# One TensorE task weighs both token halves of a head pair, and fewer halves are turned in 32x32 squares

## The chip, the cores and the metric

The kernel runs on one core of a Trainium2 chip. The metric is the time of one execution on the device, in microseconds (us); the time of the kernel before is the median of three runs, and beside it stands one profiled execution, whose rows are read here. Engines are named as in the profile: PE (matmuls), PEld (its weight loads), DVE, ACT, POOL, and SP, which here only issues DMAs (its queue is SPq).

## The reference, cut to what matters

Eight sequences of 512 tokens by 256 channels go through a decoder layer in float32: a linear attention with an MLP, a cross attention over a context of 512 rows by 128 channels, and a feed-forward block that picks one of eight adapters per sequence; a layer norm closes each. The change is in the cross attention only:

```python
qh = (q @ Wq).reshape(B, N, NUM_HEADS, HEAD_DIM).transpose(0, 2, 1, 3)   # 16 heads of 64
scores = jnp.einsum('bhnd,bhmd->bhnm', qh, kh) * scale                   # 512 tokens x 512 context rows
attn = jax.nn.softmax(scores, axis=-1)
out = jnp.einsum('bhnm,bhmd->bhnd', attn, vh)                            # the weighing
return out.transpose(0, 2, 1, 3).reshape(B, N, INNER) @ Wo + bo
```

## The kernel before, in words

**Tiling.** The batches run one after another, overlapped: while batch b is in cross attention, the linear attention and MLP of batch b+1 and the feed-forward block of batch b-1 fill the engines. In `cross_attention` the 16 heads are eight pairs (`pr`), and the tokens of a batch are two halves of 256 (`half`), each two chunks of 128 (`c`). A half of a pair is called a part here: there are 8 x 8 x 2 = 128 parts.

**One part** (`attend`, `soft`, `place`, `weigh`). For each chunk, PE makes the scores of the two heads (L872, 64-row operands, kind "rows"), DVE takes the maximum (L879), ACT the exponential (L887), and POOL or ACT scales by the inverse sum (L898, L896). The probabilities `p` stand with tokens on the partitions, and the weighing needs context rows there, so they are turned, in one of two ways:

- by PE: four 128x128 transposes for each chunk and head into a PSUM bank (L918, kind "full"), then a copy from the bank into `pT` by ACT (L371) or DVE (L373). A part takes 16 transposes and 4 copies;
- "in squares": DVE turns 32x32 blocks into `blk` (L908, 4 instructions a part), and 16 DMAs on SP's queue (L938, `place`) put the blocks in their places in `pT`. The list `BLOCKED` (L57 to L60) names these parts.

Then `weigh` multiplies `v2` by `pT`: for each of four context tiles and two heads one matmul with 64 output rows (L954, kind "cols"; 16 records a part, two for each matmul), into 256 columns of a bank `av`, which ACT or DVE copies to `oT` (L371, L373). `project_out` (L970) uses four pairs of `oT` at a time.

**Which parts are in squares before.** Batch 0 none; batches 1 to 3 the second half of each pair, 8 parts; batches 4 to 6 that and the first half of the odd pairs, 12 parts; batch 7 the first nine of such a list, which leaves its pairs 6 and 7 to PE. That is 24 + 36 + 9 = 69 parts; the other 59 are turned by PE. Batch 0 handles its two halves in two separate passes over the pairs (`part` is one half at a time).

**What sets the order.** Every piece of work is a `task` with an engine, an estimated cost, a due time and the buffers it reads and makes. `play` runs a model of the five engines when the program is built: whenever the model's engine is free, the ready task with the lowest due time is emitted, with a surcharge or rebate where PE changes its kind (`CHANGE`, `SWAY`). A task is ready only if a spot is free for each buffer that it makes. So each engine's order is fixed in the program, and on the chip each engine goes through its list in that order. Due times count in `PACE` = 3.2 us; a pair has eight of them in batches 1 to 7.

**The buffers around the change.** There are four one-bank PSUM buffers (`bank`), eight `p`, two `pT` and two `blk`. The second of `pT` and of `blk` shares memory with the product buffers of the linear attention (L251 to L254):

```python
room("pT", 1, [P, 2 * NT * 2 * P])
room("blk", 1, [P, 2 * NT * 2 * P])
for name, i in (("blk", 0), ("pT", 2)):
    rooms[name].append(Spot(prods[:, i * N : i * N + 2 * NT * 2 * P], tuple(rooms["prod"][i : i + 2])))
```

In the profile that memory is called `prods`, whatever lies in it; "bank<-prods,v" on L954 is a weighing from the second `pT`.

Of the kernel before, what the change touches and what calls it, by code (L numbers as in the profile page):

```python
# [18 lines left out]
P = 128  # L19
B, S, C = 8, 512, 256  # L20
NT = S // P
# [6 lines left out]
H2, D2 = 16, 64  # L28
INNER = H2 * D2
NPAIR = H2 // 2  # L30
# [21 lines left out]
PACE = 3200.0  # L52
# [2 lines left out]
WINDOWS = {1: (4, 44), 2: (44, 88), 3: (88, 138)}  # L55

BLOCKED = {  # L57
    b: [(pr, half) for pr in range(NPAIR) for half in range(2) if half or b > 3 and pr % 2] for b in range(1, B)
}
BLOCKED[B - 1] = BLOCKED[B - 1][:9]  # L60

AFTER = {6: (30, 84)}

# [5 lines left out]
def decoder(ctx: ExitStack, tc: tile.TileContext, t: dict, out: bass.AP):  # L69
    nc = tc.nc  # L70
# [45 lines left out]
    def task(  # L116
        engine, took, due, emit, reads=(), writes=(), weights=(), kind=None, slack=0.0, holds=(), after=0.0, others=(),
        two=False,
    ):
        k = Task(engine, took, due, emit, kind, slack)  # L120
        k.two = two
        k.on.update((e, (n, wait)) for e, n, wait in others)
        k.at = max([after] + [eta[n] for n in weights])
        before = {}
        for key in reads:
            writers, readers = last.setdefault(key, ([], []))
            before.update((id(d), d) for d in writers)
            readers.append(k)
        for key in writes:
            writers, readers = last.get(key, ([], []))  # L130
            before.update((id(d), d) for d in (*writers, *readers))
            last[key] = ([k], [])
        before.pop(id(k), None)
        for d in before.values():
            d.next.append(k)
        k.unmet = len(before)
        k.vals = list({id(v): v for v in (*(v for v, _ in (*reads, *writes)), *holds)}.values())
        k.makes = [v for v in {id(v): v for v in (*(v for v, _ in writes), *holds)}.values() if v.room]
        for v in k.vals:
            v.left += 1  # L140
        if not k.unmet:
            for e in k.on:
                ready[e].append(k)
        return k
# [118 lines left out]
    for spot_v in rooms["v"]:  # L263
        nc.gpsimd.memset(spot_v.t[:, D1, :], 1.0)

    eta = {"now": 2000.0 + 4.0 * S * C / 185}

    def arrive(name, shape):

# [92 lines left out]
    def mm(cols, n):  # L362

        return n * {512: 858.0, 256: 432.0, 128: 222.0}[cols]
# [4 lines left out]
    def copy(e, dst, src):  # L369
        if e == "act":  # L370
            nc.scalar.copy(dst, src)  # L371
        else:
            nc.vector.tensor_copy(dst, src)  # L373
# [93 lines left out]
    def chunks(v, cs=range(NT)):  # L467
        return [(v, (kc, c)) for kc in range(KC) for c in cs]
# [340 lines left out]
    def attend(b, x1T, ctx, pr, part, at):  # L809
        cols, cs = slice(pr * P, (pr + 1) * P), range(2 * part[0], 2 * part[-1] + 2)  # L810
        rows = slice(cs[0] * P, (cs[-1] + 1) * P)
        n = len(cs) * P
        qT, kT, v2, oT = Val("qT"), Val("kT"), Val("v2"), Val("oT")
        ps_q, ps_k, ps_v = Val("bank"), Val("bank"), Val("bank")

        def project_q():
            for kc in range(KC):
                nc.tensor.matmul(  # L818
                    ps_q.t[:, :n], Wq[:, kc, cols], x1T.t[:, kc, rows], start=kc == 0, stop=kc == KC - 1
                )  # L820

        def project_v():
            for m in range(NT):
                keys = slice(m * P, (m + 1) * P)
                nc.tensor.matmul(ps_v.t[:, keys], ctx.t[:, keys], Wv[:, 0, cols], start=True, stop=True)  # L825

        task("pe", mm(n, 2), at - 9 * PACE, project_q, chunks(x1T, cs), [(ps_q, 0)], ("Wq",), "full", holds=[qT])
        task(
            "act", 600, at - 8.8 * PACE, lambda: nc.scalar.mul(qT.t[:, rows], ps_q.t[:, :n], D2**-0.5),  # L829
            [(ps_q, 0)], [(qT, 0)],  # L830
        )
        task(
            "pe", mm(512, 1), at - 8 * PACE,
            lambda: nc.tensor.matmul(ps_k.t, Wk[:, 0, cols], ctx.t, start=True, stop=True),
            [(ctx, 0)], [(ps_k, 0)], ("Wk",), "full", holds=[kT],
        )
        task(
            "act", 590, at - 7.8 * PACE, lambda e: copy(e, kT.t, ps_k.t), [(ps_k, 0)], [(kT, 0)],
            others=[("dve", 690, 1500)],
        )  # L840
        task("pe", mm(128, 4), at - 3 * PACE, project_v, [(ctx, 0)], [(ps_v, 0)], ("Wv",), "full", holds=[v2])
        task(
            "act", 600, at - 2.5 * PACE,
            lambda e: copy(e, v2.t.rearrange("p m d -> p (m d)"), ps_v.t), [(ps_v, 0)], [(v2, 0)],
            others=[("dve", 690, 1500)],
        )
        for half in part:
            pT, base = Val("pT"), at + 4 * (half - part[0]) * PACE
            blk = Val("blk") if (pr, half) in BLOCKED.get(b, ()) else None
            for c in (2 * half, 2 * half + 1):  # L850
                soft(qT, kT, pT, blk, c, base + (0.1 * (c % 2) - 6) * PACE, base + 2 * (c % 2) * PACE)
            if blk:
                place(pT, blk, base + PACE)
            weigh(v2, pT, oT, half, bool(blk), base + 6 * PACE)
        return oT

    def by_head(pT):

        return pT.t.rearrange("p (m i n) -> p m i n", m=NT, i=2)

    def by_block(pT):

        return pT.t.rearrange("p (m g i n) -> p m g i n", m=NT, g=4, i=2)
# [65 lines left out]
    def place(pT, blk, due):  # L929

        keys = [(i, c) for i in range(2) for c in range(2)]

        def emit():
            to = pT.t.rearrange("p (m g r) -> p m g r", m=NT, g=4)
            of = blk.t.rearrange("p (m j r) -> p m j r", m=NT, j=4)
            for j in range(4):
                for g in range(4):
                    nc.sync.dma_start(out=to[32 * j : 32 * j + 32, :, g], in_=of[32 * g : 32 * g + 32, :, j])  # L938

        task("sp", 9600, due, emit, [(blk, k) for k in keys], [(pT, k) for k in keys], slack=2500)  # L940


    def weigh(v2, pT, oT, half, blocked, due):
        av = Val("bank")

        def emit():
            for m in range(NT):
                for i in range(2):
                    cols = slice(i * D2, (i + 1) * D2)
                    if blocked:  # L950
                        to, of = av.t[cols, : 2 * P].rearrange("p (g n) -> p g n", g=4), by_block(pT)[:, m, :, i]
                    else:
                        to, of = av.t[cols, : 2 * P], by_head(pT)[:, m, i]
                    nc.tensor.matmul(to, v2.t[:, m, cols], of, start=m == 0, stop=m == NT - 1)  # L954

        task("pe", 1728, due, emit, [(v2, 0)] + [(pT, (i, j)) for i in range(2) for j in range(2)], [(av, 0)], kind="cols", holds=[oT])
        def put(e):
            to, of = oT.t[:, half * 2 * P : (half + 1) * 2 * P], av.t[:, : 2 * P]
            if blocked:
                to, of = to.rearrange("p (c g n) -> p g c n", c=2, g=4), of.rearrange("p (g c n) -> p g c n", c=2, g=4)  # L960
            copy(e, to, of)

        task("act", 370, due + 0.5 * PACE, put, [(av, 0)], [(oT, half)], others=[("dve", 424, 100)])

    def project_out(x, oTs, prs, c, due):
        ps = Val("bank")
# [177 lines left out]
    with tc.manual_schedule(engines=MANUAL):  # L1144
        task("dve", 800, PERIOD, adapter_table, (), [(chosen, 0)], after=2 * eta["now"])
        for b in range(B):
            start = b * PERIOD
# [76 lines left out]
```

## Time and profile before

| what | value |
|---|---|
| median of 3 runs | 1658.99 us (1658.43 to 1659.1) |
| profiled execution | 1659.94 us, span of its records 1658.1 us |
| mean granted PE clock | 0.978 of full speed |
| DVE busy | 1321.9 us (80%) |
| ACT busy | 1055.4 us (64%) |
| POOL busy | 1020.2 us (62%) |
| transposes of `p` on PE (L918) | 944 |
| 32x32 turns on DVE (L908) | 200 + 76 = 276, mean 687 and 690 ns |
| DMAs of `place` (L938) | 480 + 320 + 176 + 128 = 1104, median 2.0 us to landing |
| copies into `pT` or its second spot | ACT 120 + 68, mean about 600 ns; DVE 28 + 20, mean about 675 ns |

276 turns are 69 parts of four, 1104 DMAs are 69 parts of 16, and 944 transposes are 59 parts of 16, as the list says. Busy time is the union of an engine's instructions; a timeline row gives start and extent of a run of like instructions, and since matmuls are pipelined the time that PE spends on one is read from start to next start.

### The profile page before, as it was taken

Reading aid. Unit: us, or ns where it says so; the run is one execution under the profiler, and the core shown is the slowest. Engines: PE = TensorE matmul, PEld = TensorE weight load, DVE = VectorE, ACT = ScalarE, POOL = GpSimd, SP = SyncE. Lnnn points to the kernel's source line nnn. Section 1 sums busy time; section 2 is a strip of 40 time slices with the busy share of each in tenths; the row PEclk is TensorE's granted clock in tenths of the full one; section 3 lists DMA queues with packets and bytes.
Section 4 is the critical chain, followed back from the end, with each engine's and each line's share of the span. In section 5 each row is a group of like instructions: output and inputs, shape, how many; then the busy total and the mean of one; then the engine's idle time right before and its main releaser. Section 6 shows DMA issues by size and latency. Waiting matters only on the chain.

```text
span 1658.1 us, 23850 instructions
## 1 busy us (share of the span) xinstructions
PE 1561.0 (94%) x7736; PEld 919.3 (55%) x7736; DVE 1321.9 (80%) x2248; ACT 1055.4 (64%) x2318; POOL 1020.2 (62%) x821
## 2 busy tenths in 40 slices
PE   5579999999999999989999999999999999999995
PEld 3446666654665556645566555555554654654562
DVE  6887996798889898959968899788989756776554
ACT  2257776678656796657765686567666577556543
POOL 6376986786669586758747595656967331443222
PEclk8779999999999999999999999999999999999998
DMA  8000000022112211221122222242222332233300
GB/s 266 1 1 1 1 1 1 7 51 52 51 31 68 67 27 32 57 77 39 38 52 63 79 55 65 60 118 70 66 77 71 95 80 64 74 106 89 90 6 30
DMA packets 176651, 94.43 MB, mean 57 GB/s; under 512 B 19936, under 2 KB 174048, under 8 KB 176528
## 3 DMA queue, kind: packets, MB, share of 16 engines
q1 hardware_dynamic: 175760, 91.32, 20.6%
q0 software_dynamic: 768, 1.60, 0.4%
q8 instruction: 62, 1.02, 0.3%
q14 instruction: 61, 0.50, 0.1%
HBM read 16.30 MB, written 4.19 MB: 12 GB/s over the span
## 4 chain that ended last, share of the span: by engine, by line
PE 64%; DVE 17%; ACT 6%; SPq 5%; issue 4%; POOL 2%; DMA 2%; DVEq 0%; POOLq 0%; ACTq 0%
PE bank L954 10%; PE sc L872 10%; PE bank L970 5%; PE bank L687 5%; SPq L938 5%; PE bank L712 5%; PE bank L918 5%; PE bank L818 4%; DVE nmax L879 4%; PE bank L514 3%; DVE o L612 3%; PE bank L825 2%; ACT p L887 2%; PE bank L992 2%; DVE kv L589 2%
## 5 line engine op out<-in xcount | busy, mean ns | idle before, releaser
L887 ACT ACTIVATE p<-sc,nmax 128x512 f32<-128x512 f32 x512 | 348.5, 691 | 127.5 <-DVE nmax L879 115.8
L898 POOL TENSOR_SCALAR p<-p,rinv 128x512 f32<-128x512 f32 x300 | 209.3, 710 | 294.5 <-DVE rinv L892 275.9
L879 DVE TENSOR_REDUCE nmax<-sc 128x2 f32<-128x1024 f32 x256 | 305.3, 1212 | 69.6 <-PE sc L872 69.3
L580 POOL TENSOR_TENSOR prods<-k,v 128x1088 f32<-128x1088 f32 x115 | 288.9, 2533 | 72.8 <-DVE k L554 38.8
L603 POOL TENSOR_TENSOR prods<-q,kv 128x1088 f32<-128x1088 f32 x107 | 266.7, 2516 | 37.6 <-DVE kv L589 24.8
L872 PE MATMUL sc<-kT,qT 64*128 64x512 f32 x1024 | 267.8, 628 | 4.1 <-ACT kT L371 1.8
L589 DVE TENSOR_REDUCE kv<-prods 128x68 f32<-128x1088 f32 x120 | 152.3, 1272 | 17.8 <-POOL prods L580 17.5
L612 DVE TENSOR_REDUCE o<-prods 128x68 f32<-128x1088 f32 x128 | 161.3, 1270 | 4.6 <-POOL prods L603 4.5
L918 PEld LDWEIGHTS bank<-ident,p 128*128 128x128 f32 x944 | 106.4, 141 | 88.9 <-issue 48.6
L896 ACT ACTIVATE p<-p,rinv 128x512 f32<-128x512 f32 x212 | 143.8, 732 | 6.2 <-DVE rinv L892 6.2
L872 PEld LDWEIGHTS sc<-kT,qT 64*128 64x128 f32 x1024 | 88.1, 188 | 105.4 <-issue 79.2
L908 DVE STREAM_TRANSPOSE blk<-p 128x512 f32<-128x512 f32 x200 | 130.9, 687 | 17.0 <-POOL p L898 9.3
L918 PE MATMUL bank<-ident,p 128*128 128x128 f32 x944 | 134.6, 278 | 9.3 <-ACT qT L829 2.6
L954 PE MATMUL bank<-pT,v 128*64 128x256 f32 x1040 | 128.2, 389 | 5.7 <-DMA pT<-blk 2.7
L954 PE MATMUL bank<-prods,v 128*64 128x256 f32 x1008 | 124.4, 389 | 6.9 <-DMA prods<-prods 6.1
L818 PE MATMUL bank<-x1T,Wq 128*128 128x512 f32 (+1 forms) x288 | 124.7, 556 | 0.8 <-ACT x1T L371 0.5
L970 PE MATMUL bank<-Wo,oT 128*128 128x256 f32 x512 | 121.1, 381 | 0.0
L712 PE MATMUL bank<-projT,h 128*128 128x256 f32 x512 | 119.0, 383 | 1.3 <-ACT kT L371 0.7
L712 PEld LDWEIGHTS bank<-projT,h 128*128 128x128 f32 x512 | 94.9, 190 | 28.1 <-issue 8.3
L970 PEld LDWEIGHTS bank<-Wo,oT 128*128 128x128 f32 x512 | 94.9, 190 | 26.9 <-issue 14.6
L687 PE MATMUL bank<-xT,fcT 128*128 128x512 f32 x224 | 105.9, 600 | 2.2 <-DVE x L717 1.1
L1111 DVE SCALAR_TENSOR_TENSOR h<-bank,decb,xT 128x512 f32<-128x512 f32 x128 | 88.9, 740 | 21.7 <-PE bank L1101 20.7
(140 smaller groups left out, 2676.8 us busy)
## 6 DMA issues: line engine op xcount, KB each, us to landing
prods<-blk SPq DMA_DIRECT2D x480, 64.0 KB, 2.0
pT<-blk SPq DMA_DIRECT2D x320, 64.0 KB, 2.0
prods<-prods SPq DMA_DIRECT2D x176, 64.0 KB, 2.0
pT<-prods SPq DMA_DIRECT2D x128, 64.0 KB, 2.0
x<-in_x SPq DMA_DIRECT2D x7, 512.0 KB, 5.3
out<-x SPq DMA_DIRECT2D x7, 512.0 KB, 3.1
ctx<-in_ctxT SPq DMA_DIRECT2D x8, 256.0 KB, 3.0
fcT<-in_fcT SPq DMA_DIRECT2D x1, 1024.0 KB, 7.7
```

The costliest lines, as they stand in the source:

```text
L580: (nc.gpsimd if e == "pool" else nc.vector).tensor_tensor(pr.t.rearrange("p (d e h) -> p d e h", d=DSPLIT, h=H1), k.t[:, s : s + DSPLIT, : ...
L603: (nc.gpsimd if e == "pool" else nc.vector).tensor_tensor(pr.t.rearrange("p (h e d) -> p h e d", h=DSPLIT, d=D1), q.t[:, s : s + DSPLIT, : ...
L612: nc.vector.tensor_reduce(o.t[:, s : s + DSPLIT, :], pr.t.rearrange("p (h e d) -> p h e d", h=DSPLIT, d=D1), AX.X, ALU.add)
L712: nc.tensor.matmul(ps.t[:, :C], of(f, c), projT[:, f, :], start=f == fs[0], stop=f == fs[-1])
L818: nc.tensor.matmul(ps_q.t[:, :n], Wq[:, kc, cols], x1T.t[:, kc, rows], start=kc == 0, stop=kc == KC - 1)
L872: nc.tensor.matmul(ps.t[:, i, :], qT.t[rows, c * P : (c + 1) * P], kT.t[rows, :], start=True, stop=True)
L879: lambda: nc.vector.tensor_reduce(nmax.t, ps.t, AX.X, ALU.max, negate=True), [(ps, 0)], [(nmax, 0)],
L887: lambda i=i, p=p: nc.scalar.activation(p.t, ps.t[:, i, :], AF.Exp, bias=nmax.t[:, i : i + 1], accum_out=ssum.t[:, i : i + 1]),
L898: nc.gpsimd.tensor_scalar(p.t, p.t, rinv.t[:, i : i + 1], 1.0, ALU.mult, ALU.mult)
L918: nc.tensor.transpose(bank.t[:, m * P : (m + 1) * P], p.t[:, m * P : (m + 1) * P], ident)
L954: nc.tensor.matmul(to, v2.t[:, m, cols], of, start=m == 0, stop=m == NT - 1)
L970: nc.tensor.matmul(ps.t[:, :C], oT.t[:, c * P : (c + 1) * P], Wo[:, pr, :], start=pr == prs[0], stop=pr == prs[-1])
```

## The change

`weigh` takes all parts of a pair that `attend` handles in one call, and is called once after the loop over halves. Its PE task holds the matmuls of both halves, one half after the other, into the two 256-column halves of one bank. It is due 6 `PACE` after the base of the last half, which is when the second half's weighing was due; its first half was due 4 `PACE` sooner. Where neither half is in squares one copy takes all 512 columns of the bank to `oT`; otherwise there are two copies of 256, as before. Batch 0, whose passes have one half each, keeps one half to a task.

`BLOCKED` loses the first halves of the odd pairs in batches 4 to 6, and batch 7 keeps the second halves of pairs 0 to 5: 6 x 8 + 6 = 54 parts in squares, and 74 turned by PE. A constant that the planner's model uses for the arrival of the weights is 2100 in place of 2000 ns.

```diff
 BLOCKED = {
-    b: [(pr, half) for pr in range(NPAIR) for half in range(2) if half or b > 3 and pr % 2] for b in range(1, B)
+    b: [(pr, half) for pr in range(NPAIR) for half in range(2) if half] for b in range(1, B)
 }
-BLOCKED[B - 1] = BLOCKED[B - 1][:9]
+BLOCKED[B - 1] = BLOCKED[B - 1][:6]
...
-    eta = {"now": 2000.0 + 4.0 * S * C / 185}
+    eta = {"now": 2100.0 + 4.0 * S * C / 185}
...
-            weigh(v2, pT, oT, half, bool(blk), base + 6 * PACE)
+            todo.append((half, pT, bool(blk)))
+        weigh(v2, oT, todo, base + 6 * PACE)
...
+    def weigh(v2, oT, todo, due):
         av = Val("bank")
+        low = todo[0][0] * 2 * P
         def emit():
+            for half, pT, blocked in todo:
+                half_ = av.t[:, half * 2 * P - low : (half + 1) * 2 * P - low]
+                for m in range(NT):
+                    for i in range(2):
+                        cols = slice(i * D2, (i + 1) * D2)
+                        if blocked:
+                            to, of = half_[cols].rearrange("p (g n) -> p g n", g=4), by_block(pT)[:, m, :, i]
+                        else:
+                            to, of = half_[cols], by_head(pT)[:, m, i]
+                        nc.tensor.matmul(to, v2.t[:, m, cols], of, start=m == 0, stop=m == NT - 1)
+        keys = [(pT, (i, j)) for _, pT, _ in todo for i in range(2) for j in range(2)]
+        task("pe", 1728 * len(todo), due, emit, [(v2, 0)] + keys, [(av, 0)], kind="cols", holds=[oT])
+        plain = not any(blocked for *_, blocked in todo)
+        for half, _, blocked in todo[:1] if plain else todo:
+            n = (len(todo) if plain else 1) * 2 * P
...
+            wide = n > 2 * P
+            task("act", 587 if wide else 370, due + 0.5 * PACE, put, [(av, 0)], [(oT, h) for h, *_ in (todo if plain else [(half,)])],
+                 others=[("dve", 690 if wide else 424, 100)])
```

More of the change, by code (lines that the diff above doesn't have):

```diff
@@ L820, in project_q @@
                 )
+        todo = []
         def project_v():
@@ L940, in place @@
         task("sp", 9600, due, emit, [(blk, k) for k in keys], [(pT, k) for k in keys], slack=2500)
-    def weigh(v2, pT, oT, half, blocked, due):
+    def weigh(v2, oT, todo, due):
         av = Val("bank")
+        low = todo[0][0] * 2 * P
         def emit():
[L947 to L963, printed above, removed]
@@ new lines, in weigh, with put @@
+        keys = [(pT, (i, j)) for _, pT, _ in todo for i in range(2) for j in range(2)]
[3 more added lines that the diff above has]
+            n = (len(todo) if plain else 1) * 2 * P
+            def put(e, half=half, blocked=blocked, n=n):
+                to, of = oT.t[:, half * 2 * P : half * 2 * P + n], av.t[:, half * 2 * P - low : half * 2 * P - low + n]
+                if blocked:
+                    to, of = to.rearrange("p (c g n) -> p g c n", c=2, g=4), of.rearrange("p (g c n) -> p g c n", c=2, g=4)
+                copy(e, to, of)
+            wide = n > 2 * P
+            task("act", 587 if wide else 370, due + 0.5 * PACE, put, [(av, 0)], [(oT, h) for h, *_ in (todo if plain else [(half,)])],
+                 others=[("dve", 690 if wide else 424, 100)])
```

## The prediction

> **What bounds the kernel now.** I read the page's busy shares first, then the busy time by stretches, then PE's timeline start to start, and last the waits.
>
> ```profile
> PE 1561.0 (94%) x7736; PEld 919.3 (55%) x7736; DVE 1321.9 (80%) x2248; ACT 1055.4 (64%) x2318; POOL 1020.2 (62%) x821
> PE 64%; DVE 17%; ACT 6%; SPq 5%; issue 4%; POOL 2%; DMA 2%; DVEq 0%; POOLq 0%; ACTq 0%
> ```
>
> The first line is the busy time, the second the chain that ended last, by engine. PE carries both. The change adds PE work only where parts lose their squares, in batches 4 to 7. By the starts of L954 those batches' weighings run from 930 to 1598 us; scores and turns begin somewhat sooner, so I read the stretches from 820 (columns: PE, PEld, DVE, ACT, POOL busy, then granted PE clock, DMA share, GB/s):
>
> ```profile
> 820.00:1030.00 210.00, 207.37 (x1022) 120.16 (x1022) 178.24 (x302) 147.75 (x313) 144.58 (x112) 1.00 0.23 59
> 1030.00:1220.00 190.00, 184.12 (x880) 103.61 (x878) 163.79 (x286) 123.23 (x270) 133.94 (x102) 1.00 0.30 77
> 1220.00:1400.00 180.00, 178.35 (x874) 99.22 (x872) 133.49 (x241) 122.51 (x275) 78.19 (x84) 1.00 0.31 79
> 1400.00:1600.00 200.00, 194.56 (x1043) 111.78 (x1039) 127.08 (x238) 115.78 (x293) 72.16 (x96) 0.99 0.30 79
> ```
>
> PE is busy 764.4 of 780 us, and idle 15.6. DVE, ACT and the DMA engines have room, and more of it towards the end. So here PE time is added to and taken from the end almost one for one. The large idle pieces lie outside: 45.6 us before 125 us and 18.6 after 1600, neither of which this change touches in its work.
>
> **What a weighing costs PE.** Since the extents of pipelined matmuls overlap, I use starts:
>
> ```profile
> 912.27 1.04 PE L428 MATMUL bank<-ident,xhat 128*128 128x128 f32 x8
> 913.23 1.95 PE L954 MATMUL bank<-prods,v 128*64 128x256 f32 x16
> 915.11 1.99 PE L872 MATMUL sc<-kT,qT 64*128 64x512 f32 x8
> 917.03 0.66 PE L918 MATMUL bank<-ident,p 128*128 128x128 f32 x4
> 917.52 1.88 PE L818 MATMUL bank<-x1T,Wq 128*128 128x512 f32 x4
> 919.24 1.02 PE L834 MATMUL bank<-ctx,Wk 128*128 128x512 f32 x2
> 920.10 1.04 PE L918 MATMUL bank<-ident,p 128*128 128x128 f32 x8
> 921.07 1.95 PE L954 MATMUL bank<-pT,v 128*64 128x256 f32 x16
> ```
>
> A weighing takes 915.11 - 913.23 = 1.88 us to the next start. The eight transposes ahead of the second one take 921.07 - 920.10 = 0.97; over the whole timeline eight transposes (L428) followed by more full-array work take a median of 0.88, so entering "cols" costs 0.09. In the same way L818 takes a median of 1.72 between full-array tasks and 1.82 just after a weighing: leaving towards "full" costs 0.10. The trace even holds the changed form, once, where two weighings happen to stand together:
>
> ```profile
> 1503.38 1.95 PE L954 MATMUL bank<-pT,v 128*64 128x256 f32 x16
> 1505.16 1.90 PE L954 MATMUL bank<-prods,v 128*64 128x256 f32 x16
> 1506.98 1.99 PE L872 MATMUL sc<-kT,qT 64*128 64x512 f32 x8
> ```
>
> 1506.98 - 1503.38 = 3.60 against 2 x 1.88 = 3.76: joining saves 0.16 at the seam. The matmuls themselves are not fewer.
>
> **Part by part.**
>
> *Joining.* Batches 1 to 7 have 56 pairs, so 56 visits to "cols" go. Of the present 126 visits, 87 lead on to "rows" (scores, decoder) and 39 to "full"; 110 come from "full". Between "full" and "rows" only the 0.16 is saved, because "rows" would have to be entered from "full" anyway (L834 before L872 takes 0.95 against 0.86: the same 0.09). Between "full" and "full" it is 0.09 + 0.16 + 0.10 = 0.35. Weighted: (87 x 0.16 + 39 x 0.35)/126 = 0.22, and 56 x 0.22 = **12.3 us less**. Bounds: 56 x 0.16 = 9.0 and 56 x 0.35 = 19.6.
>
> *Turning.* 69 - 54 = 15 parts go from squares to PE: 15 x 16 = 240 transposes. Four (L918) between other full-array work take a median of 0.44 us, eight take 0.97 - 0.09 = 0.88 in the rows above: 0.11 each, so 240 x 0.11 = **26.4 us more**. The bound above is the mean busy time, 134.6 us/944 = 0.143, which counts tails that overlap: 34 us.
>
> The Trainium skill speaks against added transposes more harshly. The rows show the clock at 1.00, 1.00, 1.00 and 0.99 through stretches full of them, and 0.11 us a transpose. "TensorE: Matmul & The Clock Gate", Part 4, gives about 275 ns for a transpose within a kernel and says that transposes do not lift the clock as other matmuls do. At 275 ns each the 240 would be an estimated 66 us. The mean extent on L918, 278 ns, agrees with the page, but the starts show that the next one begins long before.
>
> *Off PE.* DVE loses 60 turns of 687 ns (41 us); 60 copies from PSUM come, at 601 ns on ACT or 678 on DVE (36 to 41 us). SP's queue loses 240 DMAs; 16 of them take 10.34 to 11.53 us on it between 1026 and 1060. Two pairs of 256-column copies become two of 512 in batch 7. All this is covered by PE, busy 98% in these stretches; without that cover the copies would cost about 0.6 us each where they end a chain, as the final pair's do: below 2 us. Bank use barely moves: 60 more for transposes, 56 fewer for weighings.
>
> *Waits taken away.* PE's waits for `place` before L954 come to 6.1 + 2.7 = 8.8 us, three events:
>
> ```profile
> PE bank L954 <- DMA prods<-prods: 6.1, 1, 6.1
> PE bank L954 <- DMA pT<-blk: 2.7, 2, 1.8
> ```
>
> In batches 4 to 6 the queue holds 12 x 10.3 = 124 us of places a batch and after it 82. Up to the whole idle time of these stretches, 15.6 us, could go; I count about 3.
>
> *Waits added.* The joined task waits for both parts, and holds both `pT` until it ends. Before, one was free for the next pair while the other was weighed. After, the next pair's 16 transposes and its `place` start only after the weighing: place 10.3 + 2.0 to landing, weighing 3.6, together 16 us, against a pair's 25.6 (batch 6 takes 1468 - 1309 us from first to last weighing, 10.6 a part). There are 9 us to spare, and PE has the next MLP and the feed-forward block to run meanwhile. But the second `pT` also needs two product buffers free at the same moment, which POOL's products (2.5 us) and DVE's sums (1.27) use until about 1300. If PE stands at a weighing, the scores and transposes queued behind stand too, and ACT and DVE after them. No row shows this coupling; by the nearest rows the least is 0 (the slack covers it) and the most 24 us (each of the 48 pairs in batches 1 to 6 waits 0.5 us, a little less than half a DVE sum); I take 3, against the 3 above.
>
> *Planner's constant.* 100 ns in a weight's modelled arrival moves nothing by itself, but any edit reshuffles the emitted order. The rows give no price; I allow a few us either way.
>
> **Sum.** 1659.9 + 26.4 - 12.3 - 3 + 3 = 1674.0 for an execution like the profiled one. That execution lay 0.95 us above the median of the runs, so **1673.0 us**, 0.8% slower.
>
> **Rivals.**
>
> *1. A new wait (slower still).* The coupled `pT` starves. For it: both spots are already in heavy use (1040 and 1008 records on L954), and one is shared with the linear attention. Against it: 9 us of slack a pair. With 24 us of idle time instead of 3: 1673 + 21 = 1694.
>
> *2. Relief (faster).* The idle 15.6 us between 820 and 1600 go, because SP and DVE no longer hold anything up, and each join saves the full 0.35 us. 1673 - 3 (the added wait) - (15.6 - 3) - (19.6 - 12.3) = 1650. It decides when savings and recovered idle time together pass the 26.4 us of transposes. For it: on the chain of waits SP's places stand for 20 us at 1516 to 1537. Against it: PE was busy 22.7 of 25 us from 1516 to 1541, so that chain had little behind it; and with the likeliest saving of 12.3, recovering all 15.6 us only just passes parity.
>
> *3. Parity.* About 10 us of the idle time recovered and joins at 0.28 (15.7 us): 1673 - 3 - 7 - 3.4 = 1659.6.
>
> *4. It doesn't join in effect.* If the present order already put weighings together, nothing would be saved: 1673 + 12 = 1685. The starts show only two such neighbours in 128, so I fold this into rival 1's side.
>
> **How the numbers follow.** Slower by the sum, 1663 to 1683: 53%. Slower still: 20%. Parity: 9%. Faster: 18%. For 8 in 10 I cut about half of each outer case: **1654 to 1692**. The slower cases' own range is 1663 to 1692. A measurement tells about 0.2% from no change (1655.7 to 1662.3): faster 0.18, same 0.09, slower 0.73.
>
> **What would show it.** L918 with 1184 transposes, still near 0.11 us start to start; 864 DMAs and 216 turns; PE busy 10 to 16 us more; runs of 32 records on L954 of 3.6 us; PE idle time between 820 and 1600 near 15 us. It is wrong if PE's busy time does not rise, if that idle time falls below 5 us (rival 2), or if PE's waits before L954 grow from 9 to tens of us (rival 1).

## The result, and the profile after

The changed kernel takes 1677.01 us (median of 4 runs, 1675.94 to 1678.61) against 1658.71 for the kernel before, run beside it: a ratio of 1.0107, interval 1.0091 to 1.0123. It is slower, 18.3 us by the medians, where 14 were forecast (1673.0). Its profiled execution took 1676.93 us, its span 1675.2, so 17.1 us more than the span of before.

The first line of the page's busy times, then the same stretches as before (columns: PE, PEld, DVE, ACT, POOL busy, granted PE clock, DMA share, GB/s), of the changed kernel:

```profile
PE 1581.0 (94%) x7976; PEld 944.5 (56%) x7976; DVE 1290.8 (77%) x2176; ACT 1078.2 (64%) x2382; POOL 1014.7 (61%) x817
```

```profile
820.00:1030.00 210.00, 206.95 (x1024) 119.76 (x1023) 172.48 (x292) 151.95 (x327) 139.74 (x103) 0.98 0.18 48
1030.00:1220.00 190.00, 187.48 (x928) 110.01 (x930) 157.61 (x269) 129.21 (x283) 129.94 (x98) 1.00 0.20 53
1220.00:1400.00 180.00, 179.97 (x934) 105.89 (x932) 118.18 (x214) 122.94 (x276) 75.08 (x79) 1.00 0.20 53
1400.00:1600.00 200.00, 197.72 (x1072) 116.62 (x1074) 118.50 (x219) 123.42 (x309) 66.96 (x93) 1.00 0.22 57
```

PE's busy time rose by 20.0 us, and its idle time from 820 to 1600 fell from 15.6 to 7.9. DVE and the DMA engines lost work. PE's granted clock is 0.98 to 1.00 there and it is busy 99%, so most of what was moved to it is paid for in time.

The joined weighing, in the changed kernel's timeline:

```profile
915.20 1.95 PE L959 MATMUL bank<-prods,v 128*64 128x256 f32 x16
916.98 1.90 PE L959 MATMUL bank<-pT,v 128*64 128x256 f32 x16
918.80 1.98 PE L818 MATMUL bank<-x1T,Wq 128*128 128x512 f32 x4
```

918.80 - 915.20 = 3.60 us, the forecast value, and 55 of the 56 joined runs of the trace take that. Two lines of the waits tell what joining did to those who wait (microseconds in total, times, longest):

```profile
DVE oT L373 <- ACT oT L371: 57.7, 26, 5.9
...
PE bank L959 <- DVE h L1123: 0.2, 1, 0.2
```

PE no longer waits for `place` at a weighing (8.8 us before). The other line is easily misread. The two halves of the bank are copied out by two instructions, often one on ACT and one on DVE. The waits put down 57.7 us of DVE's idle time to ACT's copy, where before DVE's copies to `oT` waited 10.9 us for PE and never for a copy of ACT. One of the 26 places:

```profile
421.91 1.90 PE L959 MATMUL bank<-pT,v 128*64 128x256 f32 x16
...
423.85 0.38 ACT L371 COPY oT<-bank 128x256 f32<-128x256 f32 x1 [1.78 <-PE bank L959]
424.26 0.42 DVE L373 COPY oT<-bank 128x256 f32<-128x256 f32 x1 [3.31 <-ACT oT L371]
```

In all 26, DVE's copy starts 0.03 us after ACT's has ended, although it reads other columns of the bank. But DVE had been idle since 424.26 - 3.31 = 420.95, and ACT's copy could start only when the weighing was done. Summed over the 26 places, 47.4 of the 57.7 us passed before ACT's copy began, that is, DVE waited for PE's weighing; 10.4 us are what the order of the two copies adds.

The end looks different too. Before:

```profile
1596.25 1.89 PE L970 MATMUL bank<-Wo,oT 128*128 128x256 f32 x8
1598.07 1.95 PE L954 MATMUL bank<-prods,v 128*64 128x256 f32 x16
1599.95 5.45 PE L970 MATMUL bank<-Wo,oT 128*128 128x256 f32 x24
```

After:

```profile
1610.10 1.90 PE L959 MATMUL bank<-prods,v 128*64 128x256 f32 x16
1611.92 1.98 PE L1045 MATMUL bank<-xT,wd 128*128 128x512 f32 x4
1613.74 7.07 PE L982 MATMUL bank<-Wo,oT 128*128 128x256 f32 x32
```

Before, one chunk's output projection ran ahead of the last weighing, because its half was ready; after, all four come behind it, and an adapter matmul besides. From the end of the last weighing to the end of the span it is 1658.1 - 1599.95 = 58.2 us before and 1675.2 - 1611.92 = 63.3 after. Of these 5.1 us, 3.2 are work of PE that now stands behind the last weighing in place of ahead of it (PE busy 39.5 and 42.7 us there); only 1.8 us are more idle time.

### The profile page after: what moved, and what is told of

Its sections match the earlier page's. It is cut to its first block, busy times and chain, and to the rows that moved or that the text cites. A ratio compares the mean times of both kernels' runs of the same rounds, so it can differ in the third digit from the quotient of the medians.

```text
span 1675.2 us, 23982 instructions
## 1 busy us (share of the span) xinstructions
PE 1581.0 (94%) x7976; PEld 944.5 (56%) x7976; DVE 1290.8 (77%) x2176; ACT 1078.2 (64%) x2382; POOL 1014.7 (61%) x817
## 4 chain that ended last, share of the span: by engine, by line
PE 64%; DVE 6%; ACT 2%; issue 2%; SPq 1%; DMA 0%; POOL 0%; DVEq 0%; POOLq 0%; ACTq 0%
PE bank L959 11%; PE sc L874 10%; PE bank L982 6%; PE bank L920 6%; PE bank L818 5%; PE bank L712 5%; PE bank L687 5%; PE bank L514 3%; PE bank L1113 3%; PE bank L1004 3%; PE bank L835 2%; PE bank L826 2%; DVE nmax L881 1%; ACT p L889 1%; PE bank L657 1%
## 5 line engine op out<-in xcount | busy, mean ns | idle before, releaser
L580 POOL TENSOR_TENSOR prods<-k,v 128x1088 f32<-128x1088 f32 x114 | 283.6, 2513 | 67.3 <-DVE k L554 51.3
L874 PE MATMUL sc<-kT,qT 64*128 64x512 f32 x1024 | 272.8, 630 | 7.6 <-ACT kT L371 3.1
L920 PEld LDWEIGHTS bank<-ident,p 128*128 128x128 f32 x1184 | 130.5, 141 | 92.9 <-issue 46.8
L920 PE MATMUL bank<-ident,p 128*128 128x128 f32 x1184 | 161.7, 278 | 3.5 <-DVE pT L373 1.6
L371 ACT COPY prods<-bank 128x512 f32<-128x512 f32 x196 | 106.9, 597 | 67.0 <-PE bank L920 46.7
L910 DVE STREAM_TRANSPOSE blk<-p 128x512 f32<-128x512 f32 x192 | 124.9, 687 | 13.7 <-POOL p L900 9.1
L959 PE MATMUL bank<-prods,v 128*64 128x256 f32 x1024 | 124.1, 384 | 0.2 <-DVE h L1123 0.2
L959 PE MATMUL bank<-pT,v 128*64 128x256 f32 x1024 | 124.0, 385 | 0.0
L371 ACT COPY oT<-bank 128x256 f32<-128x256 f32 (+1 forms) x86 | 30.7, 381 | 137.1 <-PE bank L959 136.4
L401 POOL TENSOR_TENSOR rs<-ve,neghalf 128x4 f32<-128x4 f32 (+2 forms) x53 | 51.1, 968 | 98.3 <-DVE ve L396 97.9
```

The lines of the kernel that those rows point to most:

```text
L580: (nc.gpsimd if e == "pool" else nc.vector).tensor_tensor(pr.t.rearrange("p (d e h) -> p d e h", d=DSPLIT, h=H1), k.t[:, s : s + DSPLIT, : ...
L874: nc.tensor.matmul(ps.t[:, i, :], qT.t[rows, c * P : (c + 1) * P], kT.t[rows, :], start=True, stop=True)
L920: nc.tensor.transpose(bank.t[:, m * P : (m + 1) * P], p.t[:, m * P : (m + 1) * P], ident)
```

## The experiments

Each ratio is to the kernel before, run on the same chip between the runs of the kernel it is compared with; the interval is the 95% one. The visits are entries of PE into the row form (scores, decoder) and the column form (weighings), counted in the order of PE's instructions. PE busy and idle (span less busy) are of the profiled execution. The runs come from several chips, on which the kernel before had medians of 1656.1 to 1658.7 us, and the span of e3, in which only the planner's constant differs, is 2.7 us below the span of before: a difference of two or three microseconds between spans decides nothing, and the ratios are the better measure.

| kernel | squares | transposes | row / column visits | PE busy | PE idle | ratio |
|---|---|---|---|---|---|---|
| before | 69 | 944 | 187 / 126 | 1561.0 | 97.1 | 1 |
| changed | 54 | 1184 | 207 / 72 | 1581.0 | 94.2 | 1.0107 (1.0091 to 1.0123) |
| e2 turn only | 54 | 1184 | 194 / 128 | 1585.9 | 91.5 | 1.0129 (1.0114 to 1.0144) |
| e14 turn, join 1 to 3 | 54 | 1184 | 201 / 104 | 1581.4 | 87.6 | 1.0076 (1.0062 to 1.0090) |
| e11 join 1 to 3 | 69 | 944 | 194 / 100 | 1557.1 | 93.1 | 0.9963 (0.9949 to 0.9976) |
| e1 join where planned | 69 | 944 | 199 / 87 | 1578.5 | 161.6 | 1.0526 (1.0511 to 1.0541) |
| e9 keep `pT` as e1 | 69 | 944 | 197 / 125 | 1586.8 | 137.7 | 1.0416 (1.0397 to 1.0436) |
| e10 e2 and keep `pT` | 54 | 1184 | 217 / 124 | 1595.4 | 103.5 | 1.0237 (1.0218 to 1.0255) |
| e5 changed, scores grouped | 54 | 1184 | 179 / 72 | 1573.7 | 95.5 | 1.0090 (1.0076 to 1.0104) |
| e6 before, scores grouped | 69 | 944 | 175 / 127 | 1560.0 | 108.3 | 1.0084 (1.0070 to 1.0098) |
| e12 last pair split | 54 | 1184 | 207 / 73 | 1580.3 | 92.7 | 1.0118 (1.0102 to 1.0133) |
| e13 more squares | 77 | 816 | 187 / 126 | 1550.5 | 100.8 | 0.9987 (0.9977 to 0.9997) |
| e3 constant | 69 | 944 | 187 / 126 | 1560.1 | 95.3 | 1.0006 (0.9997 to 1.0015) |

The price of a visit that several expectations use comes from the timeline before: entering the row or the column form from full-array work 0.09; leaving columns 0.16, and 0.10 more if full-array work follows; leaving rows 0.20 (four score records take 1.06 and not 0.86), and 0.10 more likewise.

**e2, turn only.** The kernel before with the shorter list.

```diff
-    b: [(pr, half) for pr in range(NPAIR) for half in range(2) if half or b > 3 and pr % 2] for b in range(1, B)
+    b: [(pr, half) for pr in range(NPAIR) for half in range(2) if half] for b in range(1, B)
-BLOCKED[B - 1] = BLOCKED[B - 1][:9]
+BLOCKED[B - 1] = BLOCKED[B - 1][:6]
```

> The kernel before with the shorter list of squares (54 parts) and weighings still one part each. Theory (PE's own time adds up): 240 transposes at 0.11 us are 26.4 us more, visits to the row and column forms almost as many as before (194 and 128 against 187 and 126, about 1 us), so about 1686 us. Rival 1 (fewer squares also free DVE and SP, so PE idles less): 1676 to 1680. Rival 2 (the joining is what costs, through the wait for both parts, and the turning is cheap): 1659 to 1668.

1678.6 us, 1.0129. The stretch from 820 to 1600:

```profile
820.00:1600.00 780.00, 770.78 (x3919) 447.51 (x3916) 572.15 (x1000) 518.65 (x1161) 422.36 (x390) 1.00 0.20 53
```

PE idles 9.2 us there, 6.4 less than before. In the whole span busy rose by 24.9 and idle fell by 5.6: 19.3 us; by the ratio it is 21.4 (18.9 to 23.9). It lies below the theory (27.5 with the visits) and at the upper end of the first rival (1680 us by the ratio): the transposes are paid, and fewer squares give back some idle time. The second rival, that turning is cheap, is out.

**e1, join where it can be planned.** The squares of before. A pair with both halves in squares keeps two weighings: joined, it would need both `pT` for its places and hold both `blk`, which is all there are of either.

```diff
-        weigh(v2, oT, todo, base + 6 * PACE)
+            if len(todo) == len(part) or all((pr, h) in BLOCKED.get(b, ()) for h in part):
+                weigh(v2, oT, todo, base + 6 * PACE)
+                todo = []
```

> The kernel before with its 69 parts in squares, weighings joined in the 41 pairs of batches 1 to 7 that have at most one half in squares; the other 15 pairs keep two weighings. No transposes are added. Theory (seams go, but the new order enters the row form 199 times in place of 187): column visits fall from 126 to 87; with 0.30 us for leaving rows, 0.26 for columns to full, 0.16 for columns to rows and 0.09 for entering either, 4 us less, about 1654 us. Rival 1 (0.22 us for each of 39 visits to the column form, and nothing given back): 1650. Rival 2 (joining adds waits on PE): 1660 or more, with waits ahead of the weighing above 9 us.

1743.55 us, 1.0526: 87 us more, far outside theory and first rival. The second rival named the sign, not the size. PE's waits ahead of its weighings:

```profile
PE bank L961 <- DMA pT<-blk: 20.2, 5, 9.6
PE bank L961 <- DMA pT<-prods: 13.6, 4, 6.0
```

33.8 us against 8.8 before, and the idle time as a whole rose by 64.5. The places, for their part, stand on SP's queue until a weighing gives a `pT` free. That wait in the kernel before, in e9 (the next experiment) and in e1:

```profile
SPq L938 <- PE bank L954: 67.8, 25, 9.7
SPq L941 <- PE bank L957: 214.3, 36, 17.5
SPq L942 <- PE bank L961: 306.8, 56, 18.9
```

**e9, keep `pT` only.** Separate weighings, 69 squares; in e1's 41 joined pairs the first half's `pT` is kept until the second weighing is done.

```diff
+        kept = []
...
-            weigh(v2, pT, oT, half, bool(blk), base + 6 * PACE)
+            weigh(v2, pT, oT, half, bool(blk), base + 6 * PACE, kept)
+            if len(part) == 2 and not all((pr, h) in BLOCKED.get(b, ()) for h in part):
+                kept = [pT]
...
+        task("pe", 1728, due, emit, [(v2, 0)] + [(pT, (i, j)) for i in range(2) for j in range(2)], [(av, 0)], kind="cols", holds=[oT, *kept])
```

> The kernel before with its 69 parts in squares and separate weighings, in which the first half's pT is kept until the second half's weighing is done in the 41 pairs that the join-some kernel joins. Theory (the 5% of the join-some kernel is the buffers: places wait for a pT, and PE for the places): 1.04 to 1.055. Rival (it is the joined task itself, which cannot start its first half until the second is there): 1.00 to 1.01.

1.0416, in the theory's range. Nothing is joined here, so four fifths of e1's loss comes from the kept buffers, with the order that they force on the planner. PE itself waits only 13.3 us for places ahead of its weighings here; most of the 40.6 us more idle time is put down to other releasers (14.6 us ahead of L1016, for `part` from DVE, 1.9 before), so the way from the late places to the lost time is in part argued. This is why the two edits come together: with twelve parts of 16 in squares, a joined pair starves the places of `pT`. With eight the places still stand behind the weighings, in e2 and in the changed kernel:

```profile
SPq L938 <- PE bank L954: 85.9, 24, 9.7
SPq L940 <- PE bank L959: 190.0, 39, 18.9
```

But there they come early enough: in the changed kernel no wait of PE at L959 is for a place, and all its waits there come to 0.2 us.

**e10, keep `pT` in the turn-only kernel.** As e9 on e2, in all 56 pairs of batches 1 to 7.

> The turn-only kernel (54 parts in squares, one weighing for each part), in which the first half's pT is kept until the second half's weighing is done, as the joined task keeps it; nothing is joined. Theory (keeping both buffers costs, through the order that the planner can still build: row visits rise from 194 to 217): about 7 us over turn-only by the prices of the visits, ratio 1.017 against 1.013; the difference from here to the changed kernel, some 10 us, is then the saving of the seams. Rival (eight squares a batch leave slack, so keeping costs nothing): 1.013, and the seams save only the 0.2% that lie between turn-only and the changed kernel.

1.0237, more than the theory's 1.017: keeping the buffers costs 1.1% even with eight squares a batch. Against e2 PE is busy 9.5 us more (7 were priced) and idles 12.0 more:

```profile
820.00:1600.00 780.00, 760.60 (x3831) 437.22 (x3830) 587.51 (x999) 510.36 (x1130) 389.09 (x365) 1.00 0.20 52
```

From e10 to the changed kernel, which keeps the same buffers and joins, busy time falls by 14.4 us; the prices of the visits give 13.2. About 4 of the 14.4 go with the clock, since PE is busy 45.4 us at half its clock in e10 and 37.2 in the changed kernel (the last section tells of this). So the seams are worth 10 to 14 us, about the 12.3 that were forecast, if compared at equal buffers. The other 9.3 us of that step is idle time, whose cause these two traces do not settle.

**e5, the changed kernel with scores grouped.**

```diff
-    "pe": {("full", "rows"): 2000.0, ("full", "cols"): 1000.0, ("rows", "rows"): -4000.0, ("cols", "rows"): -3000.0},
+    "pe": {("full", "rows"): 2000.0, ("full", "cols"): 1000.0, ("rows", "rows"): -8000.0, ("cols", "rows"): -3000.0},
```

> The changed kernel with one number of the planner changed, the rebate for a score or decoder task right after another (8000 in place of 4000), which lowers the visits to the row form from 207 to 179; column visits stay at 72, all else too. Theory (each visit costs PE its entry and its exit): about 10 us less than the changed kernel, 1667 us. Rival 1 (the visits are hidden, what counts is the number of matmuls and transposes): 1675 to 1678. Rival 2 (scores in larger groups hold up ACT and DVE, PE idles more): above 1678.

1.0090 against 1.0107: the intervals overlap, and 0.17% is about 3 us of the 10 expected, nearer the first rival (1.010 to 1.012) than the theory (1.005). In the profiles the spans differ by 6.0 us and PE's busy time by 7.3 (9.7 priced), but PE is busy 27.9 us at half its clock in e5 and 37.2 in the changed kernel, which by itself makes about 4.6 of the 7.3. So this run does not show that row visits cost what they were priced at.

**e6, the same edit on the kernel before.**

> The kernel before with the planner's rebate for a row task after a row task at 8000 in place of 4000: row visits 175 in place of 187, nothing else meant to change. Theory (a visit costs PE about 0.39 us): about 4.6 us less, ratio 0.997. Rival (larger groups of scores delay ACT and DVE, and PE idles): 1.000 or more.

1.0084, a miss: busy fell by only 1.0 us, and idle rose by 11.2, spread over 125 to 1600. The rival's outcome. A slightly other order can cost as much as a stage of this change, so a single kernel's difference of half a per cent is no proof of a mechanism here; the 1.1% of e10 and the steps of e14 below are of that size too.

**e11, join in batches 1 to 3 only,** with the squares of before.

```diff
-        weigh(v2, oT, todo, base + 6 * PACE)
+            if len(todo) == len(part) or b > 3:
+                weigh(v2, oT, todo, base + 6 * PACE)
+                todo = []
```

> The kernel before with its 69 parts in squares; weighings joined only in batches 1 to 3, where eight parts a batch are in squares; batches 4 to 7 weigh part by part. Theory (joining saves its seams where eight squares a batch leave the buffers slack): visits priced as before give 4.6 us less, ratio 0.997. Rival (keeping both pT costs as much in waits as the seams save, as in the turn-hold kernel): 1.000 to 1.005.

1649.93 us, 0.9963, as the theory had it (0.997). PE:

```profile
PE 1557.1 (94%) x7736; PEld 918.4 (56%) x7736; DVE 1320.2 (80%) x2228; ACT 1064.7 (65%) x2342; POOL 1012.3 (61%) x815
```

Busy is 3.9 us less than before (4.6 priced), idle 4.0 less. This version is faster than both kernels, by 0.4% against the kernel before.

**e14, the changed kernel, joined in batches 1 to 3 only.** The same edit on the changed kernel.

> The changed kernel, with its 54 parts in squares, joined only in batches 1 to 3; batches 4 to 7 weigh part by part. It tells what joining is worth in batches 4 to 7, where PE got the added transposes. Theory (joining gains in batches 1 to 3 as in the join-early kernel, 0.4%, and gives part of it back later, in the stretch after the last weighing above all): 1.0095 or less to the kernel before, against 1.0106 of the changed kernel, with 58 to 60 us after the last weighing. Rival (each join saves alike, by the prices of the visits 3.8 us are lost against the changed kernel): 1.013.

1.0076, better than the changed kernel and than the theory's bound, and 59.6 us after the last weighing. So joining is worth 1.0129 - 1.0076 = 0.53% in batches 1 to 3, and in batches 4 to 7 it costs 1.0107 - 1.0076 = 0.3% (differences of ratios, each known to about 0.15%, so the second is only just clear of them). From 820 to 1600:

```profile
820.00:1600.00 780.00, 775.19 (x3988) 452.25 (x3984) 572.56 (x1003) 528.79 (x1186) 418.26 (x387) 1.00 0.20 53
```

PE idles 4.8 us there against 7.9 in the changed kernel. Over the whole span PE's busy time is the same (1581.4 and 1581.0): what joining costs late is idle time, 6.6 us, of which 3.1 lie here and 2.3 after 1600.

**e12, the last pair split.** The changed kernel, its very last pair weighed part by part.

```diff
-        weigh(v2, oT, todo, base + 6 * PACE)
+            if len(todo) == len(part) or (b, pr) == (B - 1, NPAIR - 1):
+                weigh(v2, oT, todo, base + 6 * PACE)
+                todo = []
```

> The changed kernel with the last pair of the last batch weighed part by part, all other pairs joined. Theory (joining the last pair moves the first half's output projection behind the last weighing, which made the stretch from the last weighing to the end 63.3 us in place of 58.2): 3 to 5 us less than the changed kernel, ratio 1.008 to the kernel before. Rival (that stretch is set by the feed-forward chain alone): 1.0106, the same as the changed kernel.

1.0118, no gain: the rival's outcome. The edit did not do what it was meant to, since all four output projections still stand behind the last weighing (32 records on one run), and that stretch still takes 63.5 us. It says that splitting one pair is not enough to bring the output projection forward.

**e13, more squares.** The kernel before, odd first halves in squares from batch 2 on (`b > 1` in place of `b > 3`).

> The kernel before, weighings separate, with the odd pairs' first halves in squares in batches 2 and 3 too: eight more parts, 128 fewer transposes on PE (816 against 944). Theory (each transpose is 0.11 us of PE, and PE is the bound): 14 us less, ratio 0.991. Rival (DVE, busy 87 to 92 percent there beside the linear attention, and SP's queue become the bound, as with the joined kernel that kept its squares): 1.00 to 1.03.

0.9987: PE's busy time fell by 10.5 us, and idle rose by 3.7 in the profile; by the medians about 2 us are left. Between theory and rival. Removing transposes pays less than their PE time here. That DVE, near its limit beside the linear attention, is the reason was not tried by itself.

**e3 and e4, controls.** The planner's constant alone, and the changed kernel once more.

```diff
-    eta = {"now": 2000.0 + 4.0 * S * C / 185}
+    eta = {"now": 2100.0 + 4.0 * S * C / 185}
```

> The kernel before with the planner's arrival constant at 2100 ns alone; a handful of instructions near the start change places or buffers. Theory: no difference, 1658.7 us within 0.2%. Rival (an order that is only slightly shuffled costs or gains microseconds): 1652 or 1665.

> The changed kernel itself, on the same chip and between the same runs of the kernel before as the other three. Expected 1.0107 times the kernel before, the ratio measured first, within 0.0015.

1.0006 (0.9997 to 1.0015): no difference. And 1.0106 (1.0090 to 1.0123) for the changed kernel on another chip.

## Why the prediction was right, and where its terms were off

- **The bound.** Right. PE is busy 99% from 820 to 1600, and the priced PE time (visits and 0.11 us a transpose) agrees with the measured change of busy time: 21.5 and 20.0 for the changed kernel, 27.5 and 24.9 for turn-only, 34.7 and 34.4 for e10. The others come within 5 us, except e9 and e1, where PE waits longest: 5.3 and -4.4 priced, 25.8 and 17.5 measured. Two of the signs named in advance were missed: busy time rose by 20.0 us where 10 to 16 were named, and idle time between 820 and 1600 fell to 7.9 us where it was to stay near 15.
- **Turning, 26.4 us.** The PE time was right (24.9 with two visits more to columns and seven to rows), its effect smaller: 19.3 us by the spans of e2, 21.4 by the ratios. The step "I count about 3" of recovered idle time was mis-sized: 6.4 us went between 820 and 1600, of the 15.6 that could. And of the 8.8 us of waits for `place` that it listed, 6.1 came at 725 us, ahead of the batches that lose squares; e2 still waits 5.8 us there.
- **Joining, -12.3 us.** The seam is right: 3.60 us a joined run, 72 column visits. The sum is not: e2 to the changed kernel is -0.2% by the ratios (within their intervals), -2.2 us by the spans, of which PE's busy time is -4.9 and its idle time 2.7 more. The step that failed is the count that took all other visits as fixed. The planner enters the row form 207 times and not 194, which by 0.39 a visit costs 5. Keeping both `pT` is enough to bring this about: e10, which keeps them and joins nothing, has 217. The prediction allowed a few microseconds for a reshuffled order, but had no term for this.
- **The sum.** It came within about 4 us of the measurement partly by luck: by the spans, turning cost 7 us less than its term and joining saved 10 less, and the two errors have opposite signs.
- **The added wait.** I took 3 us of 0 to 24. At PE's weighings it is not there. That the mechanism exists is shown by SP's queue, which stands 190.0 us behind weighings in the changed kernel and 85.9 in e2; what it would cost with the squares left as they were, by e9 (1.0416) and e1 (1.0526). My slack of 9 us a pair counted one place a pair; before, most odd pairs of batches 4 to 7 had two.
- **"All this is covered by PE."** Not tested by itself. DVE's copies to `oT` stand 57.7 us in 26 places where ACT's copy ends last, but only 10.4 us of it are due to that copy, and DVE is not the bound. In e14, where joining is confined to batches 1 to 3, the 57.7 us are 16.8, and the time is lower; that the one causes the other was not tried. Why joining adds 6.6 us of idle time on PE in batches 4 to 7 stays open.
- **The constant.** Nothing, as said (e3).
- **Rivals.** Relief did not decide: about half of the idle time between 820 and 1600 went (15.6 to 7.9 us), not all, and joins did not save 0.35 each. A starved `pT` is what would have come had the squares stayed.

## What to carry to other kernels

On an engine that is busy 99%, a saving at the seams between its forms is real, but it must be counted over the whole order: a planner that loses one kind of seam may add another. Joining two tasks joins their buffers' lifetimes too; test that by keeping the buffers without joining, since in e9 that price was 4.2%, where all seams together were priced at 0.7%. And where a change brings a gain and a loss in different stages, try each stage alone: here joining in three of seven batches, with the squares left as they were, gives 0.9963.

## What the runs showed of the hardware

Waits on PE cost more than their length. In e1, where PE idles most, two of its stretches:

```profile
900.00:980.00 80.00, 79.62 (x400) 47.67 (x398) 64.20 (x118) 53.84 (x108) 52.47 (x46) 1.00 0.28 73
...
1460.00:1540.00 80.00, 63.33 (x297) 35.96 (x296) 43.28 (x82) 35.23 (x86) 27.80 (x35) 0.91 0.31 82
```

Where PE is busy 79.6 of 80 us the granted clock is 1.00; where it is busy 63.3 it is 0.91. Three weighings of the second stretch, each behind a wait:

```profile
1484.43 1.95 PE L961 MATMUL bank<-pT,v 128*64 128x256 f32 x16 [2.83 <-DMA pT<-blk]
...
1498.36 2.41 PE L961 MATMUL bank<-pT,v 128*64 128x256 f32 x16 [4.06 <-DMA pT<-prods]
...
1529.08 3.68 PE L961 MATMUL bank<-pT,v 128*64 128x256 f32 x16 [5.98 <-DMA pT<-prods]
```

The same 16 records take 1.95 us after a wait of 2.83 us, as they do without one, 2.41 after 4.06 and 3.68 after 5.98. Over the span e1 has a clock of 0.963 against 0.978 before. In the traces' record of the granted clock, which in these runs holds only 1.00 and 0.50, PE has half its clock for 127.7 us of e1 and for 73.6 us before, and it is busy in 71.5 and 39.5 of them. By an estimate from these figures, 32 us more of work at half the clock are 16 us lost, nearly all of the 17.5 us by which PE's busy time is higher although it has no matmul more and fewer visits. The Trainium skill, "TensorE: Matmul & The Clock Gate", Part 1, says that the clock falls to half after an idle window of about 3.4 us; the three weighings above agree with that, but no run here measures the window itself.

A transpose of 128x128 in float32 takes PE 0.11 us in a run of them (0.44 for four), with the clock at 1.00, though its own extent is 278 ns.
